# The second image's attention: four pieces of its preparation ahead of the loop, the other 20 one per slot of the first query tile

## The chip, the cores and the metric

The kernel runs on one core of one Trainium2 chip. The metric is the device time of one execution in microseconds (us). TensorE (PE), VectorE (DVE), ScalarE (ACT), GpSimd (POOL) and the DMA-issuing SyncE (SP) each work through their own instructions in order and wait for each other with semaphores.

## The reference

Two images of 256 channels and 64 x 64 = 4096 positions go through two layers, each with a residual. Layer 0 is a state-space block with an MLP and is not touched by the change. Layer 1 is attention over the positions, on a group-normalised input:

```python
def _L1_conv_ref(x, qkv_w, qkv_b, num_heads):     # 8 heads of 32
    qkv = jnp.einsum('bchw,oc->bohw', x, qkv_w) + qkv_b[None, :, None, None]
    q, k, v = ...                                  # each (b, heads, 32, n), n = 4096
    attn_logits = jnp.einsum('bhci,bhcj->bhij', q, k) * scale
    attn_weights = jax.nn.softmax(attn_logits, axis=-1)
    out = jnp.einsum('bhij,bhcj->bhci', attn_weights, v)

x = x + _L0_conv_ref(_gn(x), ...)                  # layer 0
x = x + _L1_conv_ref(_gn(x), qkv_w, qkv_b, 8)      # layer 1
```

All is float32.

## The kernel before

The kernel runs `mamba_stage` for both images, and then `attention_block` for image 0 and for image 1. Q, K and V of image 0 are made inside `mamba_stage`, where a planner gives each engine its order; image 0 enters `attention_block` with `prepared` true and only loads. Image 1 makes its own in `prepare()`. Its order, like that of the attention loop, is written by hand.

**Preparation.** The 4096 positions are 8 tiles of T = 512. For a tile t, x is loaded (`load_x`), normalised on DVE (`normalise`, L979) and multiplied by the weights: a key piece and a query piece (`project`, L989, four float32 matmuls of 512 columns each, which the trace shows as 8 passes) and a value piece (`project_values`, L1012, eight of 256 columns, 16 passes). In all there are 24 pieces, K0, Q0, V0 to K7, Q7, V7. Each piece fills one PSUM tile of two banks, given by `s_tile()`. For keys and queries each of the two banks (m = 0, 1) is emptied by ACT, which adds the bias and rounds (`halves`, first half, L999), and then by DVE, which makes the rest that rounding left (second half, L1000); SP then stores the two to a tensor in DRAM, `qk_dram` (L1003). Values are copied by DVE (L1019) into `v`, which stays on the chip. Keys and queries are loaded back from DRAM in the layout that the attention needs (`load_keys`, `load_queries`: two DMAs of 512 KB, four of 256 KB). `group_norm_scales` ahead of it is a chain of tiny instructions over DVE, TensorE and ACT (L36 to L51).

**Attention.** Four heads make a group, and there are two groups. A query tile i is one group and 512 queries, 16 of them per image. For each, the loop goes over 32 chunks c of 128 keys. One step of this loop is a slot s = 32 i + c. In a slot the code issues: the two exponentials of s on ACT (L1099), one for each pair of heads; the value matmuls of s - 1 (L1120, into `po`); the logits of s + 1 (L1086, into two tiles from `s_tile()`); and the additions for the softmax's denominators, which are shared by DVE and POOL (`add_up`). DVE adds up the first pair of heads in chunks: one reduction over several slots (`sum_chunk`, L1112) at c = 3, 6, 9 and so on. DVE also adds a part of the second pair in the slots of the list `SHARED`. Keys of chunk c come from tile c // 4. `finish(i)` normalises and stores a query tile during the slots of the next one; for the last tile of an image nothing follows that could run beside it.

`s_tile()` has three buffers of two banks each. They serve the logits and, during the preparation, the pieces. There are nine buffers for key tiles: a pool `kp` of eight, and one in the pool `kq` that is opened after the preparation has closed its own pool. The pools p1 and p3 for small tiles are opened after the preparation as well.

The order of the preparation:

```python
for t in range(NT):
    project(t, 1)
    if t + 1 < NT:
        normalise(t + 1)
    project(t, 0)
    project_values(t)
    load_x(t + 2)
```

Nothing of the attention loop is issued before this loop is through; the first logits stand behind V7 on TensorE.

Of the kernel before, what the change touches and what calls it, by code (L numbers as in the profile page):

```python
# [11 lines left out]
F32 = mybir.dt.float32  # L12
# [7 lines left out]
P = 128  # L20
T = 512
# [892 lines left out]
def attention_block(ctx, tc, b, stats, consts, w, out, scratch, range_t, prepared):  # L914
# [25 lines left out]
    nc.gpsimd.memset(ones, 1.0)  # L940
    v = wp.tile([P, NC, C], F32, name="v")
    p2 = ctx.enter_context(tc.tile_pool(name=f"l1p2{b}", bufs=2))
    kp = ctx.enter_context(tc.tile_pool(name=f"l1k{b}", bufs=NT))
    ep = ctx.enter_context(tc.tile_pool(name=f"l1e{b}", bufs=5))
    ec = ctx.enter_context(tc.tile_pool(name=f"l1c{b}", bufs=2))
    keys = {}
    queries = {}

    def load_keys(g, t):


        k = keys[g, t] = (kq if g and t == 0 else kp).tile([P, 4, T], F32R, name="k")
        load_stack(nc, k, scratch.qk[b * KG + g, 1, t], 1)

    def load_queries(i):
        if i < KG * NT:
            g, t = divmod(i, NT)
            q = queries[i] = p2.tile([P, 4, T], F32R, name="q")
            load_stack(nc, q, scratch.qk[b * KG + g, 0, t], 0)

    def s_tile():
        return ps_s.tile([P, 2, T], F32, name="s", tag="s")

    def prepare():

        with tc.tile_pool(name=f"l1p{b}", bufs=2) as pp:
            w_qkv = pp.tile([P, KC, 3 * C], F32, name="w_qkv", bufs=1)
            nc.sync.dma_start(w_qkv, w["qkv_wT"].rearrange("(k p) f -> p k f", p=P))
            gn = group_norm_scales(nc, pp, ps_s, "s", stats, gmat, eps_t)
            xn = {}  # L970

            def load_x(t):
                if t < NT:
                    xn[t] = pp.tile([P, KC, T], F32, name="xn")
                    nc.sync.dma_start(xn[t], x.rearrange("(k p) l -> p k l", p=P)[:, :, bass.ts(t, T)])

            def normalise(t):
                for c in range(KC):
                    nc.vector.tensor_scalar(  # L979
                        xn[t][:, c, :], xn[t][:, c, :], gn[c][:, 0:1], gn[c][:, 1:2], ALU.subtract, ALU.mult  # L980
                    )

            def project(t, i):


                pm = s_tile()
                for m in range(KC):
                    for c in range(KC):
                        nc.tensor.matmul(  # L989
                            pm[:, m, :],  # L990
                            lhsT=w_qkv[:, c, bass.ds(i * C + m * P, P)],
                            rhs=xn[t][:, c, :],
                            start=(c == 0),
                            stop=(c == KC - 1),
                        )
                halves = pp.tile([P, 2, KC, T], F32R, name="halves")
                for m in range(KC):
                    bias = b_qkv[:, i * KC + m : i * KC + m + 1]
                    nc.scalar.activation(halves[:, 0, m, :], pm[:, m, :], AF.Identity, bias=bias)  # L999
                    nc.vector.scalar_tensor_tensor(  # L1000
                        halves[:, 1, m, :], pm[:, m, :], bias, halves[:, 0, m, :].bitcast(F32), ALU.add, ALU.subtract
                    )
                    nc.sync.dma_start(  # L1003
                        scratch.qk[b * KG + m, i, t].rearrange("s c h t -> (c h) s t"), halves[:, :, m, :].bitcast(F32)
                    )

            def project_values(t):
                pm = s_tile()
                flat = pm.rearrange("p a t -> p (a t)")
                for j in range(T // P):  # L1010
                    for c in range(KC):
                        nc.tensor.matmul(  # L1012
                            flat[:, bass.ts(j, C)],
                            lhsT=xn[t][:, c, bass.ts(j, P)],
                            rhs=w_qkv[:, c, 2 * C : 3 * C],
                            start=(c == 0),
                            stop=(c == KC - 1),
                        )
                nc.vector.tensor_copy(v[:, bass.ts(t, T // P), :].rearrange("p s c -> p (s c)"), flat)  # L1019

            with tc.manual_schedule():
                load_x(0)
                load_x(1)
                normalise(0)
                for t in range(NT):
                    project(t, 1)
                    if t + 1 < NT:
                        normalise(t + 1)
                    project(t, 0)
                    project_values(t)  # L1030
                    load_x(t + 2)

                    if t == 1:
                        load_queries(0)
                    if t > 0:
                        load_keys(0, t - 1)
                load_keys(0, NT - 1)

    def load_prepared():
        def load_values(g, t):  # L1040
            cs = bass.ts(t, T // P)
            nc.sync.dma_start(v[:, cs, g * P : (g + 1) * P], scratch.v[b * KG + g, :, cs, :])

        with tc.manual_schedule():
            load_queries(0)
            for t in range(NT):
                load_keys(0, t)
                load_values(0, t)
            for g in range(1, KG):
                for t in range(NT):  # L1050
                    load_values(g, t)

    load_prepared() if prepared else prepare()

    p1 = ctx.enter_context(tc.tile_pool(name=f"l1p1{b}", bufs=1))
    p3 = ctx.enter_context(tc.tile_pool(name=f"l1p3{b}", bufs=2))
    kq = ctx.enter_context(tc.tile_pool(name=f"l1kq{b}", bufs=1))

# [94 lines left out]
    def finish(i):  # L1155

        g, t = divmod(i, NT)
        d = tiles[i]
        cols = bass.ts(t, T)
        po = p1.tile([P, T], F32, name="po_sb")  # L1160
        nc.vector.tensor_copy(po, d.po)
        acc = d.acc
        nc.vector.tensor_add(acc[:, 2, :], d.acc_2, d.acc_p[:, 0, :])
        nc.vector.tensor_add(acc[:, 0:2, :], acc[:, 0:2, :], todo[i * NC + NC - 1].e[0])
        res = p3.tile([P, T], F32, name="res")
        nc.sync.dma_start(res, x[g * P : (g + 1) * P, cols])
        yield 3
        ps = ps_2.tile([P, T], F32, name="sums_ps", tag="a2")
        for h in range(4):
            part = acc[:, h, :] if h < 3 else d.acc_p[:, 1, :]  # L1170
            nc.tensor.matmul(ps[h * D : (h + 1) * D, :], lhsT=ones, rhs=part, start=True, stop=True)
        yield
        sums = p1.tile([P, T], F32, name="sums")
        nc.vector.tensor_copy(sums, ps)
        yield
        at = b * KG * NT + i
        nc.vector.tensor_reduce(range_t[:, 0, at : at + 1], sums, AX.X, ALU.max)
        yield 2
        r = p1.tile([P, T], F32, name="r")
        for j in range(T // P):  # L1180
            nc.vector.reciprocal(r[:, bass.ts(j, P)], sums[:, bass.ts(j, P)])
            yield 2
        nc.vector.tensor_reduce(range_t[:, 1, at : at + 1], r, AX.X, ALU.max)
        nc.gpsimd.tensor_mul(po, po, r)  # L1184
        yield 2
        bias = b_qkv[:, 2 * KC + g : 2 * KC + g + 1]
        nc.vector.scalar_tensor_tensor(res, po, bias, res, ALU.add, ALU.add)  # L1187
        nc.sync.dma_start(out[g * P : (g + 1) * P, cols], res)

    with tc.manual_schedule():  # L1190
        logits(0, 0)
        logits(0, 1)
        s = 0
        while s <= S or side.waiting:
            i, c = divmod(s, NC)
            if s < S:
                if c == 0:
                    tiles[i] = Slot()
                    load_queries(i + 1)
                if i % NT == NT - 1 and i < KG * NT - 1 and c % (T // P) == 0:  # L1200

                    load_keys(i // NT + 1, c * P // T)
                exponentials(s, 0)
                exponentials(s, 1)
            if 1 <= i <= KG and not prepared:
                nc.sync.dma_start(scratch.v[b * KG + i - 1, :, c, :], v[:, c, (i - 1) * P : i * P])
            if 0 < s <= S:
                values(s - 1)
                if c == 0:
                    side.start(side.now, finish(i - 1))  # L1210
            side.run()
            logits(s + 1, 0)
            logits(s + 1, 1)
            if s < S:
                add_up(s)
            s += 1


# [175 lines left out]
```

## Time and profile before

| what | us |
|---|---|
| median of 3 runs | 4530.0 (4528.72 to 4538.78) |
| profiled execution, its own time | 4532.59 |
| profiled execution, its span | 4530.8 |

| point in the profiled execution | us from the span's start |
|---|---|
| result of image 0's last query tile written by DVE | 3277.20 |
| first matmul of piece K0 of image 1 | 3286.02 |
| first logits of image 1 | 3381.76 |
| value matmuls of slot 0 (start of slot 1) | 3386.25 |
| start of slot 20, at 2.18 us a slot | 3427.7 |

Over the whole span TensorE is busy 94%, DVE 87%, POOL 84% and ACT 83%. These shares are means over stages: layer 0 to 2121 us, the attention of image 0 from 2135 to 3277, then preparation and attention of image 1. In the profile a row gives the source line, the engine, the operation, the tile written and the tiles read, how many there were, and the mean duration; "idle before" names what released the engine.

### The profile page before, as it was taken

How to read it: one execution, taken by the hardware profiler on the slowest of the kernel's cores; microseconds unless marked ns; L12 is line 12 of the kernel's file. 1: busy time of each engine (PE TensorE's matmuls, PEld its weight loads, DVE VectorE, ACT ScalarE, POOL GpSimd, SP SyncE). 2: the span in 40 equal slices, each digit the busy share in tenths (PEclk: the TensorE clock that was granted, in tenths of full speed). 3: DMA queues.
4: the chain of work that ended last, by engine and by line, in shares of the span. 5: the costliest groups of instructions: out<-in, count | busy, mean ns of one | idle time of the engine just before them, and what ended most of it. 6: DMA issues, size and time to landing. Idle time of an engine off the chain costs nothing. (4 is left out here: it accounts for less than half of the span.)

```text
span 4530.8 us, 53988 instructions
## 1 busy us (share of the span) xinstructions
PE 4248.6 (94%) x18530; PEld 1638.8 (36%) x18530; DVE 3931.0 (87%) x3316; ACT 3762.3 (83%) x4836; POOL 3821.2 (84%) x2251
## 2 busy tenths in 40 slices
PE   5799989999899999988999999999899999999998
PEld 2233333333333333333333333333343333333333
DVE  4999989999999899994889889898848898898988
ACT  4788888888788888883999999999739999999997
POOL 2999999999999999994888888888708888888887
PEclk8899999999999999999999999999999999999999
DMA  5233333333443344444311040110091100401100
GB/s 191 96 118 114 108 111 121 126 126 126 143 153 124 127 131 135 153 156 106 88 26 26 20 100 17 26 29 20 20 267 40 45 24 22 101 17 26 28 20 8
DMA packets 172938, 389.24 MB, mean 86 GB/s; under 512 B 24048, under 2 KB 50416, under 8 KB 164464
## 3 DMA queue, kind: packets, MB, share of 16 engines
q1 hardware_dynamic: 172656, 385.73, 28.0%
q8 instruction: 147, 2.41, 0.2%
q14 instruction: 135, 1.11, 0.1%
HBM read 292.34 MB, written 93.32 MB: 85 GB/s over the span
## 5 line engine op out<-in xcount | busy, mean ns | idle before, releaser
L1112 DVE TENSOR_REDUCE chunk<-chunk 128x1024 f32<-128x4096 f32 x288 | 1269.9, 4409 | 226.7 <-ACT chunk L1099 226.7
L1099 ACT ACTIVATE chunk<-s 128x1024 f32<-128x1024 f32 x992 | 1116.7, 1126 | 181.2 <-PE s L1086 146.9
L1153 POOL TENSOR_TENSOR acc_p<-acc_p,e 128x1024 f32<-128x1024 f32 x480 | 1153.0, 2402 | 135.2 <-ACT e L1099 114.1
L1086 PE MATMUL s<-q,k 128*128 128x512 f32 x4096 | 1225.6, 421 | 17.5 <-DMA v<-v_dram 14.8
L820 POOL TENSOR_TENSOR h<-h,c 128x1024 f32<-128x1024 f32 x512 | 1206.5, 2368 | 38.4 <-ACT state L817 27.8
L1120 PE MATMUL po<-chunk,v 128*32 128x512 f32 x3968 | 1114.6, 640 | 0.0
L1120 PE MATMUL po<-e,v 128*32 128x512 f32 x4224 | 1079.0, 605 | 0.0
L1099 ACT ACTIVATE e<-s 128x1024 f32<-128x1024 f32 x1056 | 1069.5, 1016 | 7.4 <-PE s L1086 7.0
L1086 PEld LDWEIGHTS s<-q,k 128*128 128x128 f32 x4096 | 689.8, 188 | 1021.5 <-issue 926.4
L803 ACT ACTIVATE da<-dt_rep,neg_a 128x512 f32<-128x512 f32 x1024 | 690.5, 701 | 118.6 <-DVE h L814 87.7
L1151 POOL TENSOR_TENSOR acc_p<-acc_p,e 128x512 f32<-128x512 f32 x480 | 631.2, 1315 | 161.4 <-ACT e L1099 138.6
L814 DVE TENSOR_TENSOR_SCAN h<-da,state,dbu 128x512 f32<-128x512 f32 x512 | 650.3, 1273 | 52.0 <-POOL dbu L809 45.9
L814 DVE TENSOR_TENSOR_SCAN h<-da,state,bn 128x512 f32<-128x512 f32 x512 | 647.4, 1265 | 12.4 <-POOL dt L595 0.5
L809 POOL TENSOR_TENSOR dbu<-dtu_rep,b 128x512 f32<-128x512 f32 x384 | 486.8, 1279 | 30.8 <-DMA dtu_rep<-dtu_dram 27.9
L234 ACT ACT_TABLE_LOAD x338 | 433.7, 1283 | 6.8 <-PEq L1384 0.7
L425 PE MATMUL bn<-proj,pick 112*128 112x512 f32 x512 | 309.2, 617 | 111.3 <-DVE h L814 111.1
L846 PE MATMUL y<-h,sum 128*32 128x512 f32 x2048 | 358.8, 638 | 24.4 <-POOL h L820 24.0
L809 DVE TENSOR_TENSOR bn<-dtu_rep,bn 128x512 f32<-128x512 f32 x512 | 349.1, 682 | 30.6 <-PE bn L425 16.2
L1150 DVE TENSOR_TENSOR acc<-acc,e 128x512 f32<-128x512 f32 x448 | 309.8, 691 | 24.3 <-ACT e L1099 13.8
L1120 PEld LDWEIGHTS po<-chunk,v 128*32 128x32 f32 x3968 | 142.9, 108 | 360.7 <-issue 349.6
L425 PE MATMUL mm<-yn,w_in 128*128 128x512 f32 x512 | 250.4, 615 | 12.3 <-ACT yn L514 9.3
L425 PE MATMUL mm<-xm,taps 128*128 128x512 f32 x512 | 237.1, 606 | 11.1 <-POOL xm L561 8.7
(135 smaller groups left out, 4068.4 us busy)
## 6 DMA issues: line engine op xcount, KB each, us to landing
dt_rep<-dt_dram SPq DMA_DIRECT2D x128, 512.0 KB, 5.0
dtu_rep<-dtu_dram SPq DMA_DIRECT2D x128, 512.0 KB, 5.5
q<-qk_dram SPq DMA_DIRECT2D x128, 256.0 KB, 4.8
k<-qk_dram SPq DMA_DIRECT2D x64, 512.0 KB, 8.1
b<-bc_dram SPq DMA_DIRECT2D x64, 256.0 KB, 3.1
c<-bc_dram SPq DMA_DIRECT2D x64, 256.0 KB, 4.6
dt_dram<-dt SPq DMA_DIRECT2D x64, 256.0 KB, 2.1
dtu_dram<-lw SPq DMA_DIRECT2D x64, 256.0 KB, 3.4
```

Source lines behind the costliest of these rows:

```text
L234: self.nc.scalar.preload_act_table_set(self.TABLES[task.table])
L425: nc.tensor.matmul(out, lhsT=lhsT, rhs=rhs, start=(i == 0), stop=(i == len(pairs) - 1))
L803: nc.scalar.activation(da[j].tile, dt.tile[:, j, :], AF.Exp, scale=scale)
L809: engine.tensor_mul(out.tile, dtu.tile[:, j, :], rows.tile)
L814: nc.vector.tensor_tensor_scan(h.tile[:, j, :], da[j].tile, dbu.tile, initial, ALU.mult, ALU.add)
L820: nc.gpsimd.tensor_tensor(h.tile, h.tile, rows_c.tile.unsqueeze(1).to_broadcast([P, 2, T]), ALU.mult)
L1086: nc.tensor.matmul(ps[:, j, :], lhsT=keys[i // NT, kt][:, h, kj : kj + P], rhs=queries[i][:, h, :], start=True, stop=True)
L1099: nc.scalar.activation(e, todo[s].s[half], AF.Exp, scale=SCALE)
L1112: nc.vector.tensor_reduce(out, terms, AX.XY, ALU.add)
L1120: nc.tensor.matmul(tiles[i].po[h * D : (h + 1) * D, :], lhsT=v[:, c, g * P + h * D : g * P + (h + 1) * D], rhs=todo[s].e[h // 2][:, h % 2, :],
L1151: nc.gpsimd.tensor_add(acc_p[:, 1, :], acc_p[:, 1, :], eb[:, 1, :])
L1153: nc.gpsimd.tensor_add(acc_p, acc_p, eb)
```

## The change

The preparation becomes a generator that yields after each piece's matmuls. Four pieces (K0, Q0, V0, K1) are issued ahead of the attention loop. Each slot ends with one `next(steps)`: it empties the PSUM tile of the piece before, and issues the next piece's matmuls. Slot 0 takes V1, slot 19 takes Q7, and slot 20 empties it. The order of the pieces is K0, Q0, V0, K1, then V(t), K(t+1), Q(t) for each t.

The value pieces are copied out by ACT instead of DVE. `halves` becomes a tile for one bank with three buffers, where it was a tile for both with two. The load of key tile t is issued three pieces after piece K(t); K7's after all others. The second query tile's load moves from slot 0 to slot 8, for both images. The pools p1 and p3 open ahead of the preparation. `kp` has seven buffers and `kq` two. The reciprocals of `finish` are written over the sums. In the changed program's instruction order the group-norm chain, the load of the weights and the first two loads of x stand among the last instructions of image 0, ahead of its last two outputs on SP.

```diff
-    kp = ctx.enter_context(tc.tile_pool(name=f"l1k{b}", bufs=NT))
+    kp = ctx.enter_context(tc.tile_pool(name=f"l1k{b}", bufs=NT - 1))
...
+    p1 = ctx.enter_context(tc.tile_pool(name=f"l1p1{b}", bufs=1))
+    p3 = ctx.enter_context(tc.tile_pool(name=f"l1p3{b}", bufs=2))
...
+        def store(t, i, pm):
+            for m in range(KC):
+                halves = pp.tile([P, 2, T], F32R, name="halves", bufs=3)
+                bias = b_qkv[:, i * KC + m : i * KC + m + 1]
+                nc.scalar.activation(halves[:, 0, :], pm[:, m, :], AF.Identity, bias=bias)
+                nc.vector.scalar_tensor_tensor(
+                    halves[:, 1, :], pm[:, m, :], bias, halves[:, 0, :].bitcast(F32), ALU.add, ALU.subtract
+                )
+                nc.sync.dma_start(scratch.qk[b * KG + m, i, t].rearrange("s c h t -> (c h) s t"), halves.bitcast(F32))
...
+        pieces = [(1, 0), (0, 0), (2, 0), (1, 1)]
+        for t in range(1, NT):
+            pieces += [(2, t), (1, t + 1), (0, t)] if t + 1 < NT else [(2, t), (0, t)]
+        load_x(0)
+        load_x(1)
+        normalise(0)
+        loads = []
+        for n, (i, t) in enumerate(pieces):
+            pm = s_tile()
+            if i == 2:
+                project_values(t, pm)
+                normalise(t + 1)
+            else:
+                project(t, i, pm)
+
+            if i == (0 if t else 2):
+                load_x(t + 2)
+            if loads and loads[0][0] <= n and loads[0][1] < NT - 1:
+                load_keys(0, loads.pop(0)[1])
+            yield
+            if i == 2:
+                nc.scalar.copy(v[:, bass.ts(t, T // P), :].rearrange("p s c -> p (s c)"), pm.rearrange("p a t -> p (a t)"))
+            else:
+                store(t, i, pm)
+            if i == 1:
+                loads.append((n + 3, t))
+            if (i, t) == (2, 0):
+                load_queries(0)
+                load_keys(0, loads.pop(0)[1])
+        stack.close()
+        open_keys()
+        for _, t in loads:
+            load_keys(0, t)
...
-    load_prepared() if prepared else prepare()
+    START = 4
+    steps = iter(())
+    if prepared:
+        open_keys()
+        load_prepared()
+    else:
+        steps = prepare()
+        with tc.manual_schedule():
+            for _ in range(START):
+                next(steps)
...
-        r = p1.tile([P, T], F32, name="r")
+        r = sums
...
-                    load_queries(i + 1)
+                if c == (0 if i else 2 * (T // P)):
+                    load_queries(i + 1)
...
             logits(s + 1, 0)
             logits(s + 1, 1)
             if s < S:
                 add_up(s)
+            next(steps, None)
             s += 1
```

More of the change, by code (lines that the diff above doesn't have):

```diff
@@ L942, in attention_block @@
     p2 = ctx.enter_context(tc.tile_pool(name=f"l1p2{b}", bufs=2))
-    kp = ctx.enter_context(tc.tile_pool(name=f"l1k{b}", bufs=NT))
+    kp = ctx.enter_context(tc.tile_pool(name=f"l1k{b}", bufs=NT - 1))
     ep = ctx.enter_context(tc.tile_pool(name=f"l1e{b}", bufs=5))
     ec = ctx.enter_context(tc.tile_pool(name=f"l1c{b}", bufs=2))
+    p1 = ctx.enter_context(tc.tile_pool(name=f"l1p1{b}", bufs=1))
+    p3 = ctx.enter_context(tc.tile_pool(name=f"l1p3{b}", bufs=2))
     keys = {}
     queries = {}
+    pools = {}
     def load_keys(g, t):
-        k = keys[g, t] = (kq if g and t == 0 else kp).tile([P, 4, T], F32R, name="k")
+        pool = kp if (g * NT + t) % (NT + 1) < NT - 1 else pools["kq"]
+        k = keys[g, t] = pool.tile([P, 4, T], F32R, name="k")
         load_stack(nc, k, scratch.qk[b * KG + g, 1, t], 1)
@@ L962, in s_tile, with open_keys @@
         return ps_s.tile([P, 2, T], F32, name="s", tag="s")
+    def open_keys():
+        pools["kq"] = ctx.enter_context(tc.tile_pool(name=f"l1kq{b}", bufs=2))
     def prepare():
[L966 to L977, printed above, removed]
-                for c in range(KC):
-                    nc.vector.tensor_scalar(
-                        xn[t][:, c, :], xn[t][:, c, :], gn[c][:, 0:1], gn[c][:, 1:2], ALU.subtract, ALU.mult
-                    )
[L983 to L1001, printed above, removed]
-                    )
[L1003 to L1037, printed above, removed]
@@ new lines, in prepare, with load_x @@
+        stack = ExitStack()
+        pp = stack.enter_context(tc.tile_pool(name=f"l1p{b}", bufs=2))
+        w_qkv = pp.tile([P, KC, 3 * C], F32, name="w_qkv", bufs=1)
+        nc.sync.dma_start(w_qkv, w["qkv_wT"].rearrange("(k p) f -> p k f", p=P))
+        gn = group_norm_scales(nc, pp, ps_s, "s", stats, gmat, eps_t)
+        xn = {}
+        def load_x(t):
+            if t < NT:
+                xn[t] = pp.tile([P, KC, T], F32, name="xn")
+                nc.sync.dma_start(xn[t], x.rearrange("(k p) l -> p k l", p=P)[:, :, bass.ts(t, T)])
@@ new lines, in normalise, with project @@
+        def normalise(t):
+            for c in range(KC if t < NT else 0):
+                nc.vector.tensor_scalar(
+                    xn[t][:, c, :], xn[t][:, c, :], gn[c][:, 0:1], gn[c][:, 1:2], ALU.subtract, ALU.mult
+                )
+        def project(t, i, pm):
+            for m in range(KC):
+                for c in range(KC):
+                    nc.tensor.matmul(
+                        pm[:, m, :],
+                        lhsT=w_qkv[:, c, bass.ds(i * C + m * P, P)],
+                        rhs=xn[t][:, c, :],
+                        start=(c == 0),
+                        stop=(c == KC - 1),
+                    )
@@ new lines, in store @@
+        def store(t, i, pm):
+            for m in range(KC):
+                halves = pp.tile([P, 2, T], F32R, name="halves", bufs=3)
[3 more added lines that the diff above has]
+                    halves[:, 1, :], pm[:, m, :], bias, halves[:, 0, :].bitcast(F32), ALU.add, ALU.subtract
+                )
+                nc.sync.dma_start(scratch.qk[b * KG + m, i, t].rearrange("s c h t -> (c h) s t"), halves.bitcast(F32))
@@ new lines, in project_values @@
+        def project_values(t, pm):
+            for j in range(T // P):
+                for c in range(KC):
+                    nc.tensor.matmul(
+                        pm.rearrange("p a t -> p (a t)")[:, bass.ts(j, C)],
+                        lhsT=xn[t][:, c, bass.ts(j, P)],
+                        rhs=w_qkv[:, c, 2 * C : 3 * C],
+                        start=(c == 0),
+                        stop=(c == KC - 1),
+                    )
+        pieces = [(1, 0), (0, 0), (2, 0), (1, 1)]
@@ L1051, in load_prepared @@
                     load_values(g, t)
-    load_prepared() if prepared else prepare()
-    p1 = ctx.enter_context(tc.tile_pool(name=f"l1p1{b}", bufs=1))
-    p3 = ctx.enter_context(tc.tile_pool(name=f"l1p3{b}", bufs=2))
-    kq = ctx.enter_context(tc.tile_pool(name=f"l1kq{b}", bufs=1))
+    START = 4
[8 more added lines that the diff above has]
+                next(steps)
     class Slot:
@@ L1178, in finish @@
         yield 2
-        r = p1.tile([P, T], F32, name="r")
+        r = sums
         for j in range(T // P):
-            nc.vector.reciprocal(r[:, bass.ts(j, P)], sums[:, bass.ts(j, P)])
+            nc.vector.reciprocal(r[:, bass.ts(j, P)], r[:, bass.ts(j, P)])
             yield 2
```

## The prediction

> **What bounds the kernel now.** I read the table by stages first, since the share of busy time over the whole span mixes three stages. Of its rows these matter (times in us from the span's start; per engine the busy time and the number of instructions, then the granted TensorE clock, the DMA share and GB/s):
>
> ```profile
> core 0: us, PE busy (x) PEld busy (x) DVE busy (x) ACT busy (x) POOL busy (x), PEclk, DMA share, GB/s
> 3258.00:3286.00 28.00, 11.13 (x57) 4.24 (x56) 18.18 (x28) 7.35 (x9) 7.47 (x6) 0.67 0.23 75
> 3286.00:3382.00 96.00, 89.60 (x257) 50.69 (x258) 38.28 (x53) 22.59 (x32) 0.00 (x0) 0.94 0.89 268
> ...
> 3387.00:3428.00 41.00, 41.00 (x228) 15.77 (x228) 29.84 (x12) 37.86 (x38) 36.18 (x19) 1.00 0.37 81
> ```
>
> The reader should see that TensorE is the busy engine on both sides of the change: 89.6 of 96 us in the second image's preparation, and all 41 us in the first slots of its attention. So the pieces don't move into free TensorE time. What can be won is only TensorE idleness: 16.9 us in the first row (the tail of image 0 and the start of the preparation), 6.4 in the second. ACT stands idle in the preparation (22.6 of 96), but ACT is not what ends it.
>
> Then the timeline of a slot in the attention (start, duration, engine, line):
>
> ```profile
> 3396.02 1.20 PE L1086 MATMUL s<-q,k 128*128 128x512 f32 x4
> 3396.79 1.11 ACT L1099 ACTIVATE chunk<-s 128x1024 f32<-128x1024 f32 x1 [0.15 <-PE s L1086]
> 3397.15 0.65 PE L1120 MATMUL po<-chunk,v 128*32 128x512 f32 x2
> ...
> 3397.79 1.00 ACT L1099 ACTIVATE e<-s 128x1024 f32<-128x1024 f32 x1
> 3397.93 4.42 DVE L1112 TENSOR_REDUCE chunk<-chunk 128x1024 f32<-128x4096 f32 x1 [2.12 <-ACT chunk L1099]
> 3398.20 1.20 PE L1086 MATMUL s<-q,k 128*128 128x512 f32 x4
> ```
>
> From one L1086 to the next is 2.18 us, a slot. ACT waits 0.15 us for TensorE in it, TensorE waits for nothing: TensorE sets the slot. The first exponential starts 0.77 after its logits do. One 4.42 us reduction on DVE comes every third slot.
>
> Last, the timeline of the preparation:
>
> ```profile
> 3313.03 0.69 ACT L999 ACTIVATE halves<-s,b_qkv 128x512 fp32r<-128x512 f32 x1 [4.69 <-PE s L989]
> ...
> 3313.76 0.75 DVE L1000 SCALAR_TENSOR_TENSOR halves<-s,b_qkv,halves 128x512 fp32r<-128x512 f32 x1 [2.98 <-ACT halves L999]
> ...
> 3314.54 0.69 ACT L999 ACTIVATE halves<-s,b_qkv 128x512 fp32r<-128x512 f32 x1 [0.82 <-DVE halves L1000]
> ...
> 3315.26 0.75 DVE L1000 SCALAR_TENSOR_TENSOR halves<-s,b_qkv,halves 128x512 fp32r<-128x512 f32 x1 [0.76 <-ACT halves L999]
> ...
> 3319.67 7.03 PE L989 MATMUL s<-xn,w_qkv 128*128 128x512 f32 x16
> ...
> 3326.54 3.62 PE L1012 MATMUL s<-w_qkv,xn 128*128 128x256 f32 x16
> ...
> 3332.31 8.77 PE L989 MATMUL s<-xn,w_qkv 128*128 128x512 f32 x16 [2.16 <-DVE xn L979]
> ```
>
> A key and a query piece together take 3326.54 - 3319.67 = 6.87 us, so 3.44 each; a value piece takes the same. Emptying a piece's PSUM tile is a chain of four, ACT, DVE, ACT, DVE, each waiting for the one before: 3313.03 to 3316.01, 3.0 us. The last line is a pair after TensorE had waited 2.16 us: 8.77 instead of 7.03, its first passes ran at half speed.
>
> **What the Trainium skill says.** "TensorE: Matmul & The Clock Gate", Part 1, says that the array falls to half its clock after an idle window of about 3.4 us and needs about as long to return; the trace agrees with the halving (8.77 against 7.03) already after 2.16 us, while another wait of 2.04 us cost nothing. "PSUM — Partial Sum Buffer", section on bank collisions, says that two engines must not touch one bank at once, so ACT and DVE can't read the same half in parallel; the trace has them one after the other, 0.04 us apart. "ScalarE: Activation LUTs", Table sets, says that copy and identity are in every set: I count no table load for ACT's new work among the exponentials. "Perfetto Trace Analysis", Optimization Strategy, recommends interleaving regimes whose busiest engine differs; here it is the same one.
>
> **The change part by part.** In the changed program's instruction order a slot has on PE: values(s-1), logits(s+1), a piece; on ACT: two exponentials, then the emptying of the piece before; on DVE: the slot's reduction or addition, then the emptying. The score tiles have three PSUM buffers; two go to the logits, so a piece waits for the emptying of the piece before it.
>
> *Start.* The weight load and two loads of x now stand on SP ahead of the last two outputs of image 0, so they are hidden in its attention. The group-norm chain no longer waits for the output's landing (before: result written 3277.2, chain from 3279.5, first piece 3286.0). I add the chain's rest behind 3277.2: copy, difference, square 0.6, TensorE 0.6, root and reciprocal 0.5, first half of normalising 0.7: first piece at 3279.6, a gain of 6.4. K0 takes 6.3 (cold, as before), Q0 3.4, V0 3.4, K1 3.4 after a DVE wait. On SP the loads of q and k stand behind the load of x[2], which waits for Q0's second store (3292 to 3295) and V0's end (3292.8): q and k are issued by about 3297. A key load lands 10.6 us after issue in the preparation, 6.5 in the quiet attention:
>
> ```profile
> k<-qk_dram SPq DMA_DIRECT2D x16, 512.0 KB, 6.5
> ```
>
> So the first logits come between 3302 and 3308; I take 3304.5. Then exponentials (0.8 + 2.1), emptying of K1 (3.0), and piece V1 (3.4, plus 2 for a cold array): values(0) starts at 3316. Before it started at 3386.25. **Gain 70.**
>
> *Pieces in slots 1 to 19.* 19 x 3.44 = **65.4 back**, all on TensorE, which has no idle time there.
>
> *The emptying.* Count from the slot's start, when the previous piece has just ended; its result is there at 0.25. TensorE has 2.18 us of other work, then wants the buffer. After a value piece ACT copies once, 128x1024; the trace has it only on DVE (1.23), the exponential's 1.0 to 1.1 on ACT is the nearest row: done at 1.4, no wait. After a key piece the chain of four ends at 3.25: a wait of 1.1 us. After a query piece the slot is always one with a reduction: it starts when the exponential of the slot ends, 3.6 into the slot before, which lasts 2.18 + 1.1 + 3.44 = 6.7, and so ends 1.3 into this slot; DVE's first half then runs 1.3 to 2.05, ACT's second to 2.8, DVE's to 3.55: a wait of 1.5. In slots 12 and 18 an addition (0.69) stands between: 2.2. Sum: 6 x 1.1 + 3 x 1.5 + 2 x 2.2 = **15.5** (slot 3 apart). Lower bound, if the second half did not wait for DVE: 6.
>
> *Slot 3.* logits(4) needs K1. Its load stands on SP behind the load of x[3], which waits for the end of piece Q1, that is for slot 3's start. Issued at 0.7 to 1.3, landing 6.5 later plus 1.8 for x's 512 KB ahead of it at 290 GB/s: 8.5 to 9.5 against a need at 1.06. **7.5** of waiting (bounds 4 and 10), and 1.5 for the half clock after it. K2 to K7 have two slots or more between load and need: nothing, as slots of 5.6 us and more cover the 10.6 of a slow load. K7, loaded after the last store, has some 16 us.
>
> *Counted at nothing:* reciprocals in place (same shape); ACT's new work (at most 2.2 us in a slot that lasts 5.6 against its 2.15); stores and x loads (3.5 MB per 19 us, 180 GB/s, where the preparation moved 268); the later load of the second query; POOL, whose additions are unchanged. If slots were shorter than 5.6, ACT would be late next.
>
> Sum: -70 + 65.4 + 15.5 + 9 = **+20 us**. The profiled execution took 4532.6 (span 4530.8), so 4552.6 for a like one; the median of the runs shown is 2.6 below, so 4550.
>
> **The rivals.** *Not slower: the stores don't hold TensorE.* If the emptying fits into the 2.18 us, as it would with DVE free and ACT's two halves back to back, 15.5 shrinks to between 0 and 6, and if K1 also lands in time, 9 goes too: -70 + 65.4 = -5, 4525; with q and k landing at 3301 and no cold V1, -10. The deciding point: 70 / 19 = 3.7 us of growth per slot, of which the piece takes 3.44. A mean wait of 0.26 us per slot ends the gain. Against it stands the chain of 3.0 us in the trace. *Much slower: the clock.* If waits of 1.1 to 2.2 us in every slot keep the array from full clock, each costs up to 4 passes x 0.43 = 1.7 more: with 13 waits, +22, 4572. Against it: 2.04 us did no harm. *The change does not do what it says*, the pieces all being run ahead: excluded by the instruction order, where 20 stand between logits.
>
> **How the numbers follow.** This kernel's runs tell about 0.2%, 9 us, from no change. Main case 0.63, 4541 to 4562, slower. Clock or later landings 0.17, to 4575, slower. Stores or keys hidden in part 0.14, 4521 to 4540, mostly within 0.2%. All of it hidden with an early start 0.06, below 4521. Leaving out some 2 in 10 at the ends gives 4534 to 4570.
>
> **What would show it.** Right: first piece near 3280, first logits near 3304; TensorE idle before each value and query piece, released by DVE's L1010; one wait of some 7 us on a key load before the fifth slot's logits; slot 20 some 20 us later than 3427.7. Wrong: slots of 5.6 us without a wait before the pieces, or first logits before 3300.

## The result, and the profile after

Over five runs each the changed kernel took 4554.92 us (4551.64 to 4558.56) and the kernel before 4533.73 us (4528.72 to 4538.78): a ratio of 1.005, 95% interval 1.0039 to 1.0062. It is slower by 21 us; the forecast was 4550, 20 above the median shown. The profiled execution of the changed kernel has a span of 4554.0 us, 23.2 above that of the kernel before.

Both timelines, read from the start of the `sums_ps` matmuls in the tail of image 0 (3268.33 before, 3267.34 after), give the account by section:

| section | before | after | difference | predicted |
|---|---|---|---|---|
| `sums_ps` to first piece | 17.69 | 11.19 | -6.5 | -6.4 |
| first piece to first logits | 95.74 | 28.07 | -67.7 | -70.8 |
| first logits to slot 1 | 4.49 | 12.47 | +8.0 | +7.0 |
| slot 1 to slot 20 | 41.41 | 131.59 | +90.2 | +89.9 |
| sum | 159.33 | 183.32 | +24.0 | +19.7 |

The table by stages of the changed kernel (columns as in the table of before) shows where TensorE stands idle: from the first piece to slot 1, in slot 3, and in the slots 4 to 19.

```profile
core 0: us, PE busy (x) PEld busy (x) DVE busy (x) ACT busy (x) POOL busy (x), PEclk, DMA share, GB/s
...
3278.50:3319.07 40.57, 27.52 (x65) 15.57 (x65) 6.71 (x11) 10.15 (x12) 2.34 (x1) 0.68 0.49 143
...
3331.50:3347.50 16.00, 7.94 (x29) 5.52 (x28) 3.39 (x5) 3.36 (x4) 2.35 (x1) 0.68 0.85 229
3347.50:3450.00 102.50, 91.85 (x360) 44.34 (x360) 45.91 (x41) 50.47 (x58) 29.36 (x16) 1.00 0.57 175
```

In the first two rows the granted clock is 0.68 as well: in this execution TensorE also ran at half speed for some time after its waits. From 3310 us, in slot 0, to slot 20 its waits have three causes (total, times, longest; the 8.1 is in slot 3):

```profile
PE s L1112 <- DMA k<-qk_dram: 8.1, 1, 8.1
PE s L1018 <- DVE halves L1010: 7.5, 6, 1.6
PE s L995 <- DVE halves L1010: 5.7, 6, 1.0
```

The timeline at the start, with the first keys:

```profile
3294.73 1.11 SPq L907 DMA_DIRECT2D k<-qk_dram  x2
3306.60 2.05 PE L1112 MATMUL s<-q,k 128*128 128x512 f32 x4 [10.99 <-DMA k<-qk_dram]
...
3312.73 6.40 PE L1018 MATMUL s<-w_qkv,xn 128*128 128x256 f32 x16 [1.65 <-DVE halves L1010]
```

K1 is through, and TensorE waits 10.99 us for a key load whose last issue ended at 3295.84. V1, the first piece after it, takes 6.40 us, where such a piece takes 3.62 at full speed. That is so in this execution; e1, e2 and e6 will show V1 at full speed after waits as long.

Slot 3, from the same timeline:

```profile
3331.61 0.38 SPq L984 DMA_DIRECT2D xn<-x_dram  x1
3332.09 1.11 SPq L907 DMA_DIRECT2D k<-qk_dram  x2
...
3340.70 2.05 PE L1112 MATMUL s<-q,k 128*128 128x512 f32 x4 [8.06 <-DMA k<-qk_dram]
3342.54 5.08 PE L1018 MATMUL s<-w_qkv,xn 128*128 128x256 f32 x16
```

The load of key tile 1 stands behind that of x[3], which SP could issue only when piece Q1 had ended; the logits of slot 4 wait for it. And slot 6, after query piece Q2:

```profile
3356.36 3.70 PE L995 MATMUL s<-xn,w_qkv 128*128 128x512 f32 x8 [0.95 <-DVE halves L1010]
3356.52 4.42 DVE L1138 TENSOR_REDUCE chunk<-chunk 128x1024 f32<-128x4096 f32 x1 [0.22 <-ACT chunk L1125]
3359.99 0.65 PE L1146 MATMUL po<-chunk,v 128*32 128x512 f32 x2
...
3360.15 0.69 ACT L1009 ACTIVATE halves<-s,b_qkv 128x512 fp32r<-128x512 f32 x1 [2.75 <-issue]
...
3360.87 0.75 DVE L1010 SCALAR_TENSOR_TENSOR halves<-s,b_qkv,halves 128x512 fp32r<-128x512 f32 x1
...
3361.65 0.69 ACT L1009 ACTIVATE halves<-s,b_qkv 128x512 fp32r<-128x512 f32 x1 [0.82 <-DVE halves L1010]
...
3362.37 0.75 DVE L1010 SCALAR_TENSOR_TENSOR halves<-s,b_qkv,halves 128x512 fp32r<-128x512 f32 x1 [0.76 <-ACT halves L1009]
...
3363.18 3.72 PE L1018 MATMUL s<-w_qkv,xn 128*128 128x256 f32 x16 [0.94 <-DVE halves L1010]
```

It is the chain of four that the preparation of before showed, now between two pieces: it takes 3.0 us, and TensorE has 2.2 us of other work beside it. ACT's second read is of the other bank, and still it starts only when DVE has done with the first; no run shows why.

### The profile page after: what moved, and what is told of

Same layout as the page of the kernel before. It is cut to its first block, busy times and chain, and to the rows that moved or that the text cites. A ratio compares the mean times of both kernels' runs of the same rounds, so it can differ in the third digit from the quotient of the medians.

```text
span 4554.0 us, 53983 instructions
## 1 busy us (share of the span) xinstructions
PE 4259.3 (94%) x18530; PEld 1642.7 (36%) x18530; DVE 3921.7 (86%) x3308; ACT 3767.3 (83%) x4844; POOL 3821.4 (84%) x2251
## 5 line engine op out<-in xcount | busy, mean ns | idle before, releaser
L814 DVE TENSOR_TENSOR_SCAN h<-da,state,bn 128x512 f32<-128x512 f32 x512 | 647.5, 1265 | 12.4 <-POOL dt L595 0.5
L809 POOL TENSOR_TENSOR dbu<-dtu_rep,b 128x512 f32<-128x512 f32 x384 | 487.4, 1281 | 26.3 <-DMA dtu_rep<-dtu_dram 23.6
L425 PE MATMUL mm<-yn,w_in 128*128 128x512 f32 x512 | 250.1, 615 | 11.6 <-ACT yn L514 9.2
```

Source lines behind the costliest of these rows:

```text
L425: nc.tensor.matmul(out, lhsT=lhsT, rhs=rhs, start=(i == 0), stop=(i == len(pairs) - 1))
L809: engine.tensor_mul(out.tile, dtu.tile[:, j, :], rows.tile)
L814: nc.vector.tensor_tensor_scan(h.tile[:, j, :], da[j].tile, dbu.tile, initial, ALU.mult, ALU.add)
```

## The experiments

All edits are made to the changed kernel. Four ran on one chip beside 48 runs of the kernel before (median 4532.0 us), the last two beside 33 (4529.7 us). Two columns follow the traces: slot 20 counted from the `sums_ps` matmuls of the tail, against 159.33 before. The changed kernel ran beside other runs of the kernel before (4533.73 us), so the rows are best compared by what each lies above or below the kernel before that ran beside it: +21.2, +12.0 (e1), +9.2 (e2), +9.9 (e3), +4.8 (e4), -2.2 (e6) and -8.8 us (e5).

| kernel | median us | ratio to before (95%) | to slot 20 | against before |
|---|---|---|---|---|
| changed kernel | 4554.92 | 1.005 (1.0039 to 1.0062) | 183.3 | +24.0 |
| e1, key tile 1 earlier | 4543.97 | 1.0029 (1.0018 to 1.004) | 171.8 | +12.4 |
| e2, ACT alone empties | 4541.15 | 1.0017 (1.0011 to 1.0024) | 165.9 | +6.6 |
| e3, all ahead | 4541.88 | 1.0021 (1.0013 to 1.0028) | 166.2 | +6.9 |
| e4, seven ahead | 4536.78 | 1.0008 (1.0 to 1.0016) | 160.8 | +1.5 |
| e6, e1 and e2 | 4527.5 | 0.9995 (0.9986 to 1.0003) | 155.5 | -3.9 |
| e5, e4 and e2 | 4520.89 | 0.9981 (0.9974 to 0.9988) | 149.0 | -10.3 |

**e1: the load of key tile 1 one piece earlier.**

```diff
-                loads.append((n + 3, t))
+                loads.append((n + (2 if t == 1 else 3), t))
```

> Edit: the load of key tile 1 is issued one piece earlier (slot 1), ahead of the load of x[3] on SP; nothing else. Theory (three separate costs: the key load, the emptying of PSUM, the start): TensorE's 8.1 us wait before the logits of slot 3 and the half-clock stretch after it (slot 3 took 16.05 us) shrink to the ordinary wait of a slot after a query piece, about 6.8 us for slot 3; slot 20 starts at about 3441.5 instead of 3450.7, and the time falls by 9 us, to 12 to 15 us above the kernel before. Rival (the DMA queues are full in this stretch, so that the wait only moves): slot 3 still takes over 12 us, or another load is late, and the time stays within 3 us of the changed kernel.

Slot 3 took 6.84 us instead of 16.05, and slots 4 to 19 were as in the changed kernel. Of TensorE's waits for keys only the one at the start stayed:

```profile
PE s L1112 <- DMA k<-qk_dram: 11.4, 1, 11.4
```

The median is 11 us below the changed kernel's, or 9.2 when each is set against the kernel before beside it (9 expected). The trace gives 11.6, but only 9.2 of it is slot 3. Another 2.7 is V1, which the edit does not touch: it started before the moved load was issued, and took 3.72 us instead of 6.40, though TensorE had waited as long ahead of it.

```profile
3301.68 2.05 PE L1112 MATMUL s<-q,k 128*128 128x512 f32 x4 [11.39 <-DMA k<-qk_dram]
...
3307.81 3.72 PE L1018 MATMUL s<-w_qkv,xn 128*128 128x256 f32 x16 [1.68 <-DVE halves L1010]
```

So the late load was the queue's order, not a lack of bandwidth, and the rival falls.

**e2: ACT alone reads the PSUM tile.** ACT writes the biased value into the second half, DVE rounds it into the first and subtracts in place.

```diff
-                nc.scalar.activation(halves[:, 0, :], pm[:, m, :], AF.Identity, bias=bias)
-                nc.vector.scalar_tensor_tensor(
-                    halves[:, 1, :], pm[:, m, :], bias, halves[:, 0, :].bitcast(F32), ALU.add, ALU.subtract
-                )
+                raw = halves[:, 1, :].bitcast(F32)
+                nc.scalar.activation(raw, pm[:, m, :], AF.Identity, bias=bias)
+                nc.vector.tensor_copy(halves[:, 0, :], raw)
+                nc.vector.tensor_sub(halves[:, 1, :], raw, halves[:, 0, :].bitcast(F32))
```

> Edit: ACT alone reads the PSUM tile of a key or query piece (it writes the biased value to the chip's memory); DVE makes both halves from there, so that DVE is no longer between the piece and the release of its buffer. Theory: ACT's two reads end about 1.6 us into the slot, before TensorE's 2.2 us of other work is done; the waits of 0.95 to 1.5 us ahead of 12 pieces vanish, every slot with a piece takes 5.6 us, and with the slots after key and query pieces each 1.2 to 1.8 us shorter the time falls by 12 to 15 us (the slot 3 wait for the key load stays), to 7 to 11 us above the kernel before. Rival (the waits come from ACT being late, or from the stores' DMAs that hold the three buffers of halves): the waits stay, released by ACT, and the time stays within 4 us of the changed kernel.

Slot 6 in its timeline: ACT's two reads are done 1.38 us into the slot (3355.84 + 1.27 = 3357.11 against a start of 3355.73), and the piece follows the logits with no wait.

```profile
3355.73 0.65 PE L1146 MATMUL po<-chunk,v 128*32 128x512 f32 x2
...
3355.84 1.27 ACT L1010 ACTIVATE halves<-s,b_qkv 128x512 f32<-128x512 f32 x2 [1.89 <-PE s L995]
...
3356.78 1.19 PE L1112 MATMUL s<-q,k 128*128 128x512 f32 x4
...
3357.80 3.62 PE L1018 MATMUL s<-w_qkv,xn 128*128 128x256 f32 x16
```

Every slot with a piece took 5.6 to 5.63 us, but for slot 3 (17.11, the key load) and slot 9 (6.01). The median fell by 13.8 us (12.0 by the kernels before beside each), to 9.2 above the kernel before, inside what was expected. The trace says 17.4: the slots give 13.0, and the stretch from first logits to slot 1 fell from 12.5 to 8.1 us, which the expectation had left out. 2.7 us of that stretch is again V1 at full speed (3.72 us), which the edit can't claim. DVE in the release of the buffer was the cause of the waits; ACT and the stores' DMAs were not. With DVE out of the way a store shows once: in slot 9 ACT's second read waits 0.8 us for the DMA that still holds `halves`.

**e3: all 24 pieces ahead.**

```diff
-    START = 4
+    START = 24
```

> Edit: all 24 pieces are issued ahead of the loop (START = 24); all other edits of the change stay. Theory (it is the placing of the pieces that costs; the earlier group norm and x loads are a gain of 6 to 7 us): the first piece starts near 3278.5, the preparation is bound by TensorE and by the three one-bank buffers of halves and takes 98 to 106 us to slot 1, and the time is between 8 us below and 3 us above the kernel before. Rival (an edit other than the placing costs: the copies on ACT, the smaller buffers, in-place reciprocals): the time stays 10 us or more above the kernel before.

It came out 9.9 us above the kernel before, outside what my theory allowed and just short of the rival's 10. From the first piece to the first logits it took 108.8 us, 13 more than before. The waits in that stretch say why it is no clean undoing:

```profile
PE s L995 <- DVE xn L988: 16.0, 5, 6.9
...
DVE xn L988 <- DMA xn<-x_dram: 10.4, 5, 3.2
ACT halves L1009 <- DMA qk_dram<-halves: 7.5, 3, 5.0
```

TensorE waits for normalised x, and DVE for the load of x. By the order of the code, Q(t) now comes after K(t+1), so the two buffers of x are held longer and the next x is late; and ACT waits for stores that hold the three one-bank buffers of `halves`. Which of the two makes x late was not separated, so for what the placing costs e4 to e6 have to speak. Part of the rival e3 does settle: from slot 1 to slot 20 it took 42.5 us, against 41.4 before, and from there to the last `po<-chunk` matmuls every trace, that of before included, took 1081.6 to 1081.7 us. The reciprocals over the sums, the key pools and the later query load cost nothing there.

**e4: seven pieces ahead.** The same line with `START = 7`.

> Edit: seven pieces ahead of the loop instead of four (START = 7). Theory: V1, K2 and Q1 run in the 11 us in which TensorE waited for the first keys and queries, so three slots shrink by 3.44 each (10), V1 is no longer cold (3), key tile 1 is loaded before the loop needs it (9), and two waits for the emptying go (2.4): 20 to 26 us below the changed kernel, within 5 us of the kernel before; first logits still at 3306 to 3309. Rival (the stores of the three extra pieces delay the first keys and queries by as much as is won): first logits at 3314 or later, and the time no more than 12 us below the changed kernel.

First logits came 28.3 us after the first piece, as with four ahead (28.07), with three more pieces done by then; TensorE's wait for the first keys fell from 10.99 to 0.8 us. Slot 3 took 6.84 us. The median is 18 us below the changed kernel's (20 to 26 expected) and 4.8 above the kernel before, the trace gives 22.5 and +1.5. The rival's delay did not come. The stretch from first logits to slot 1 stayed at 12.25 us, though V1 was no longer in it: another value piece, V2, stands in its place. It waited 1.67 us for the emptying of the piece before it and then took 5.68 us, slow as V1 had been, although TensorE's longest wait just before was 1.7 us. So the 3 us counted for V1 were not won.

**e6 and e5: two edits in one kernel.** e6 has the edits of e1 and e2.

> Edit: four pieces ahead as in the changed kernel, key tile 1 loaded one piece earlier, and ACT alone reads the PSUM tiles. Theory: all slots with a piece take 5.6 us, slot 3 too; what stays against the kernel with seven pieces ahead is the 11 us of idle TensorE before the first logits; slot 20 starts 143 us after the first piece, the time is 1 to 6 us below the kernel before and 22 to 28 below the changed kernel. Rival (the savings overlap): 8 us or more above the kernel before.

Slot 20 started 155.5 us after the tail's `sums_ps`: 27.9 below the changed kernel, where e1 and e2 alone give 11.6 + 17.4 = 29.0. Both of these contain V1's 2.7 us, which can be won only once; without it they give 26.3. The savings do not overlap; e6 has even 1.6 us more, in part because in e2 the wait in slot 3 had been 1 us longer. All slots with a piece took 5.6 us but for slot 9 (6.15), where ACT's second read again waited 1.0 us for a store's DMA. The median, 2.2 us below the kernel before, can't be told from it (0.9986 to 1.0003).

e5 has `START = 7` and the edit of e2.

> Edit: seven pieces ahead, and ACT alone reads the PSUM tiles of key and query pieces, in one kernel. Theory (the start, the key load and the emptying are separate costs, and without them the pieces in the slots cost only their own TensorE time): every slot with a piece takes 5.6 us, slot 1 starts 8 us after the first logits instead of 12, slot 20 starts 133 us after the first piece (before 141.6, changed kernel 172.1), and with the first piece some 6.5 us earlier the time is 10 to 16 us below the kernel before, that is 32 to 38 below the changed kernel. Rival (the savings overlap, since one stall hides another): no more than 25 us below the changed kernel, within 4 us of the kernel before.

Its slots with a piece took 5.6 us but for slots 3 and 9 (6.12 and 5.96), in which ACT's second read waited 0.9 and 0.8 us for a store's DMA. From 3310 us to slot 17 TensorE waited twice, the first time ahead of slot 1, which starts at 3316.47:

```profile
PE s L1112 <- ACT e L1125: 0.5, 1, 0.5
PE s L1018 <- ACT halves L1010: 0.2, 1, 0.2
```

The time is 8.8 us below the kernel before (0.9981, interval 0.9974 to 0.9988) and 34 below the changed kernel (30.0 by the kernels before beside each); 10 to 16 below the kernel before had been expected. First logits to slot 1 took 10.9 us instead of the 8 counted, which is most of what is missing: V2 took 6.06 us there. It is the fastest version of the study.

## Why the prediction was right

*TensorE on both sides.* Right. TensorE's share does not change with the place of a piece: in e2, e5 and e6 a slot with a piece takes 5.6 us, 2.18 + 3.44, and all but one or two have nothing left to wait for (slot 9 in each, slot 3 in e5; e2 keeps the key load in slot 3). Even then the gain is only 8.8 us, from idleness removed. (ACT's 22.6 of 96 us in the preparation is its busy time, not its idle time.)

*The start.* The group norm and the x loads were hidden as worked out (6.5 us for 6.4): before, DVE waited 2.26 us for the output's landing and 1.26 us for x ahead of the first piece, and in the changed kernel for neither. Mis-sized was the landing of the first keys: I took 3304.5, between the quiet 6.5 and the busy 10.6 us; counted from the first piece it was 28.07 instead of 24.9, the slow end. The cold V1 cost 2.8 us (6.40 against 3.62) instead of 2. The term came true partly by luck: in e1, e2 and e6, after waits of 11.0 to 11.6 us, V1 took 3.72.

*The emptying.* Predicted 15.5, measured from the lengths of the slots: (6.82 - 5.62) x 6 after key pieces, 1.22 x 3 after query pieces and 1.8 x 2 where the addition stands between: 14.5. The term too large was the query piece's, 1.5 against 1.2 (2.2 against 1.8 with the addition): the reduction ended 0.95 us into the slot, not 1.3 (3356.52 + 4.42 against slot 6's start at 3359.99), so that it hardly touched the chain. That DVE in this chain is the cause is shown by e2.

*Slot 3.* Predicted 7.5 of waiting and 1.5 of half speed, 9 in all; measured 8.06 and 16.05 - 5.62 = 10.4 in all. The 290 GB/s taken for x's load lies between the 268 of the preparation and the 296 of its last stretch, 3382 to 3387 us. Beside the wait, the logits at half speed (2.05 us against 1.20) and V2 (5.08 against 3.62) make the rest. The cause, the place on SP, is shown by e1.

*The rivals.* The deciding point, 0.26 us of waiting per slot, was passed with (131.59 - 41.41 - 65.4) / 19 = 1.3 us. What "stores and keys hidden" would give was put at 4525; e6, which hides both, ran 2.2 us below the kernel before, in line with the -5 worked out there. The clock did not drop after the waits of 0.95 to 1.5 us: it is 1.00 in the row from 3347.5 on.

*The sum.* The trace's sections give +24.0 against +19.7: the first keys (+3.1), slot 3 (+1.4) and the start of slot 1 (+1.0) were put too low, the emptying (-1.0) too high. That the median came within 1 us of the forecast is partly luck.

*What was counted at nothing.* It stayed at nothing: no table load stands on ACT in the slots 0 to 20 of the changed kernel, the last one being ahead of the first exponential, and after slot 20 the changed kernel runs as before (1081.6 us to the last `po<-chunk` matmuls, in both).

*Open:* medians and traces differ by up to 3.3 us, either way (changed kernel +21.2 against +24.0, e4 +4.8 against +1.5). The scatter of single executions is larger: the tail's `sums_ps`, which come before all that e1 to e6 edit, start between 3262.1 and 3270.1 us in the profiled executions. What decides whether V1 runs at half speed stays open too.

## What to carry to other kernels

Work moved into a loop whose busy engine is the one it needs costs its full time there; what it can win is idle time of that engine, so count that first and set it against every new wait. A piece that shares a small pool of PSUM tiles with the loop has to be emptied within the time of the loop's own work: keep the release on one engine that has room, and let the others work from a copy. And put enough pieces ahead of the loop to cover the round trip of its first operands through DRAM.

## What the runs showed of the hardware

A wait of TensorE can cost again as half speed after it, but the same wait does not always. After a wait of 8.06 us V2 took 5.08 us, and after 10.99 and 1.65 us V1 took 6.40, against 3.62 at full speed. In e1, after 11.39 and 1.68 us, V1 took 3.72; the granted clock from the first logits to slot 1 was 0.53 in the changed kernel and 0.78 in e1. Waits of 0.95 to 1.5 us in two slots of three left a piece at 3.7 us. So one trace does not price such a stretch. And a chain over two engines is dear beside its work: the same two banks were emptied by ACT alone in 1.27 us, by ACT and DVE in turn in 3.0.
